# Two attention layers on one core: all softmax divisions on ScalarE, and the sums of the output weights spread out

## The chip, the cores and the metric

The kernel runs on one core of a Trainium2 chip. A core has TensorE (PE, matrix products), VectorE (DVE), ScalarE (ACT), GpSimd (POOL) and SyncE (SP, which here only issues transfers), and 16 DMA engines that they share. The time is the device time of one execution in microseconds (us); lower is better. The engines run on their own and wait for one another through semaphores.

## The reference

Four images of 32 x 32 positions and 768 channels go through two layers. Each layer normalizes its input in 32 groups of channels and adds the result of an attention over all 1024 positions with 12 heads of 64 channels and decomposed relative positions:

```python
qkv = x @ Wqkv                       # layer 1: + qkv_b
rel_h = einsum('bhwc,hkc->bhwk', r_q, Rh)
rel_w = einsum('bhwc,wkc->bhwk', r_q, Rw)
scores = scale * einsum('bqc,bkc->bqk', q, k) + rel_h[..., :, None] + rel_w[..., None, :]
attn = softmax(scores)
out = einsum('bqk,bkc->bqc', attn, v)
x = x + (out @ Wproj + bproj)        # x was normalized by _gn before the attention
```

## The kernel before

**Images, pairs, units.** The code counts eight images: 0 to 3 are the four inputs in layer 0, 4 to 7 the same four in layer 1 (`LAST` = 7). An image has six pairs of heads (`pair` 0 to 5; `g` counts pairs through all images), and a pair has eight units (g, n) of 128 query positions, n = 0 to 7. The main loop runs over these 384 units (`at` is the running number) and issues the work of all engines in one order written out by hand; nothing is reordered afterwards, so each engine goes through its instructions in the order of the program, and so do the DMA queues that SyncE and ScalarE issue to.

**A unit.** `biases` makes the sum of the two relative positions for both heads on POOL (L533, into `sc`, six buffers, two units ahead of use). `scores` multiplies k by q on TensorE (L547). `exponentials` subtracts them on VectorE with the row minimum (L559, `sm`) and takes the exponential and its row sum on ScalarE (L563). `divide` makes the reciprocal of the row sum on VectorE (L571) and multiplies `sc` by it, one instruction per head: on ScalarE (L577), or, for the first head of n = 2 and n = 4, on POOL (L575), except in the very last pair. `turn` transposes blocks on VectorE (L583) and writes the result to DRAM (`td`, L585). `read_back` fetches it again with keys on the partitions (`pt`, L594), two or three iterations later. `weigh` multiplies `pt` by v on TensorE (L612, `av`): for units 0 to 3 of a pair at n = 6, for units 4 to 7 at n = 2 of the next pair. An iteration issues the scores and the division of the next unit, the biases of the unit after that and the transpose of its own.

**Between them.** The pieces of the products for q, k, v and the output (`products`, `values`, `out_product`, L354, L382, L438, L701) are put into the units by `plans`. They are seven-product forms of 2 x 2 block products, so sums of weights and of inputs are needed: `combine` and `combine_values` (L135, L146), `sums` for the next image (L323, in pair 4 from n = 4 and in pair 5) and `out_sums` (L691), all on POOL. `complete` loads the residual, adds it on POOL (L758) and stores the result one iteration later from SyncE (L762). Relative positions go through DRAM (`tdr`) and come back as `rel` (L518).

**The sums of the output weights.** For each layer l and each of three column blocks o, `combined` loads the four blocks of the output weight from DRAM (L635), makes four differences on POOL (L640) and stores them in DRAM tables (L649), from where `fetch_out` reads them for every image (L675). With b11, b12, b21, b22 for the four blocks, table 1 is b12 - b11, table 2 is b22 - (table 1), table 3 is b22 - b12 and table 4 is b21 - (table 2). `combining` says at which unit each stage is issued: loads (stage 0) and stores (stage 3) at the top of the iteration, ahead of that iteration's read-backs and `td`; the subtractions (stages 1 and 2) near its end:

```python
    for k in range(LAYERS * NB):
        for stage in range(4):
            combining.setdefault(NT + 4 * k + stage + (stage > 0), []).append((k // NB, k % NB, stage))
```

With NT = 8 and NB = 3 these are six blocks, four units apart: block k has its loads at unit 8 + 4k, its subtractions two and three units later and its stores four units later, where the loads of block k + 1 come too. The first tables are needed in pair 4 of image 0, those of layer 1 in pair 4 of image 4. Loaded weights lie in `unit` buffers, of which there are 35, used also by inputs, attention outputs and residuals.

Of the kernel before, what the change touches and what calls it, by code (L numbers as in the profile page):

```python
# [31 lines left out]
FP = mybir.dt.float32  # L32
AF = mybir.ActivationFunctionType
ALU = mybir.AluOpType
ENGINES = {getattr(mybir.EngineType, e) for e in ("PE", "DVE", "Activation", "Pool", "SP")}

P = 128
# [4 lines left out]
NT = S // P  # L42
# [4 lines left out]
LAYERS = 2  # L47
NP = NH // 2
FULL = 2 * HW - 1
BIG = 3.0e38  # L50
NB = NC // 2
# [6 lines left out]
def attention_blocks(ctx: ExitStack, tc: tile.TileContext, a: dict, out: bass.AP):  # L58
    nc = tc.nc
# [15 lines left out]
    dram = ctx.enter_context(tc.tile_pool(name="scratch", bufs=1, space=bass.MemoryType.DRAM))  # L75
# [11 lines left out]
    NPAIR = NI * NP  # L87

    def unit(name):

        return upool.tile([P, HALF], FP, tag="u", name=name)
# [69 lines left out]
    for sign, base in ((1, 0), (-1, GS // NC - 1)):  # L161
        nc.gpsimd.affine_select(
            out=same_group, in_=same_group, pattern=[[-sign * (GS // NC), NG], [0, GS // NC]],
# [4 lines left out]
    for l in range(LAYERS):  # L168
        tab = const.tile([P, 2, 2 * HW], FP, tag=f"tab{l}", name=f"tab{l}")
        nc.gpsimd.memset(tab, 0.0)  # L170
        for i, ax in enumerate("hw"):
            src = a[f"rel{ax}{l}"]
            n = src.shape[1]
# [21 lines left out]
    for l in range(LAYERS):  # L195
        t = const.tile([P, NC], FP, tag=f"bo{l}", name=f"bo{l}")
# [370 lines left out]

    def divide(g, n):
        st = st_of[g, n]
        last = g + 1 == NPAIR  # L570
        nc.vector.reciprocal(st[:, 2, :], st[:, 1, :])  # L571
        for h in range(2):
            sc = sc_of[g, n, h].rearrange("p k j -> p (k j)")
            if h == 0 and n in (2, 4) and not last:
                nc.gpsimd.tensor_scalar(sc, sc, st[:, 2, h : h + 1], 1.0, ALU.mult, ALU.mult)  # L575
            else:
                nc.scalar.mul(sc, sc, st[:, 2, h : h + 1])  # L577

    def turn(g, n):

# [46 lines left out]
    tables = {}  # L627

    def combined(l, o, stage, held={}):

        if stage == 0:
            tables[l, o] = dram.tile([4, P, NB * P], FP, tag=f"tw{l}_{o}", name=f"tw_{l}_{o}")
            held[l, o] = [unit(f"t{k}_{l}_{o}")[:, : NB * P] for k in range(4)]
            for k, t in enumerate(held[l, o]):
                nc.sync.dma_start(  # L635
                    out=t, in_=a[f"wo{l}"][o + k % 2 * NB][:, k // 2 * NB * P : (k // 2 + 1) * NB * P]
                )
            return
        b11, b12, b21, b22 = held[l, o]
        sub = lambda to, x, y: nc.gpsimd.tensor_tensor(to, x, y, ALU.subtract)  # L640
        if stage == 1:
            sub(b11, b12, b11)
            sub(b12, b22, b12)
        elif stage == 2:
            sub(b22, b22, b11)
            sub(b21, b21, b22)
        else:
            for k, t in enumerate((b11, b22, b12, b21)):
                nc.sync.dma_start(out=tables[l, o][k], in_=t)  # L649

    order = [
        (im, kind, o) for im in range(LAST)
# [6 lines left out]
    def fetch_out(at):  # L659

        if at >= len(order):
            if at < len(order) + 2:
                fetch(3 + 4 * (at - len(order)))
            return
        im, kind, o = order[at]
        l = images[im][0]
        raw = lambda k: a[f"wo{l}"][o + k % 2 * NB][:, k // 2 * NB * P : (k // 2 + 1) * NB * P]
        made = lambda k: tables[l, o][k - 1]
        out_weights[im, kind, o] = []
        for k, src in enumerate({  # L670
            "a": lambda: (raw(0), made(3)), "b": lambda: (raw(2), made(2)),
            "c": lambda: (made(1), made(4)), "d": lambda: (raw(3),),
        }[kind]()):
            w = wopool.tile([P, NB, P], FP, tag="wo", name=f"wo_{im}_{kind}{o}_{k}")
            nc.sync.dma_start(out=w, in_=src.rearrange("p (c o) -> p c o", o=P))  # L675
            out_weights[im, kind, o].append(w)
# [91 lines left out]
    at_start, at_sums, at_stats, here = {}, {}, {}, [0]  # L768
# [136 lines left out]
        (0, 3): (1, 1, 2), (0, 1): (1, 2, 0), (0, 2): (1, 2, 1), (0, 4): (1, 2, 2),  # L905
    }
    combining = {}
    for k in range(LAYERS * NB):
        for stage in range(4):
            combining.setdefault(NT + 4 * k + stage + (stage > 0), []).append((k // NB, k % NB, stage))  # L910
    applies = {
        1: ((0, 0), (0, 3)), 2: ((0, 1), (0, 4)), 3: ((1, 0), (1, 1), (0, 2)),
        4: ((1, 3), (1, 4), (0, 5)), 5: ((1, 2), (1, 5)),
# [10 lines left out]
    with tc.manual_schedule(engines=ENGINES):  # L924
# [40 lines left out]
        ahead["G0"].part()  # L965
        ahead["G0"].between()
        divide(0, 0)
        biases(0, 1)
        held = []
# [11 lines left out]
        for at, (g, n) in enumerate(units):  # L981
# [22 lines left out]
            if (pair, n) in streams and im + 1 < B:  # L1004
                c, i = streams[pair, n]
                x = unit(f"stream_{im + 1}_{c}_{i}")
# [4 lines left out]
            for part in combining.get(at, []):  # L1011
                if part[2] % 3 == 0:
                    combined(*part)
            if (pair, n) == (4, 0) and im == 0:
                fetch_out(0)
                fetch_out(1)
# [50 lines left out]
            if at + 1 < len(units):  # L1067
                divide(*units[at + 1])
# [10 lines left out]
            if (pair, n) in out_sum_steps:  # L1079
                back, which, c = out_sum_steps[pair, n]  # L1080
                if 0 <= im - back < LAST:
                    out_sums(im - back, which, c)
            for part in combining.get(at, []):
                if part[2] % 3:
                    combined(*part)
# [79 lines left out]
```

## Time and profile before

| | |
|---|---|
| median of 3 runs | 3297.41 us (3296.28 to 3298.17) |
| profiled execution, its own time | 3294.32 us |
| span from first to last instruction | 3292.2 us, granted clock 0.998 |
| busy: PE, DVE, ACT, POOL | 3236.3, 2581.8, 2004.3, 2668.7 us |
| data moved | 1029.63 MB, mean 313 GB/s |
| L575 (divisions on POOL) | 94, 105.3 us busy |
| L640 (differences of output weights) | 24, 24.1 us busy |
| L635 and L649 (their loads and stores) | 24 and 24, 192 KB each |

A line of a group in the page reads: line of the code, engine, operation, written tile <- read tiles, shapes, count, then busy time in us and mean time of one in ns, then the time that the engine stood idle just before these instructions and what ended most of it. A line of the waits reads: who waited <- what it waited for: us in total, times, longest. A row of windows gives, for a stretch of time, the busy time of each engine with its number of instructions, the granted clock of TensorE, the busy share of the DMA engines and their rate. In the timeline a row is start, length, engine and instruction, and in brackets the idle time before it with its releaser. Busy time of TensorE is modelled from matmuls that overlap, so a stretch that is fully busy there need not run at full pace.

### The profile page before, as it was taken

To read this page: it belongs to the slowest core of one execution; us is meant where nothing else is said; L and a number is where in the kernel's file an instruction comes from. 1 tells how busy PE (TensorE), PEld (TensorE's weight loads), DVE (VectorE), ACT (ScalarE), POOL (GpSimd) and SP (SyncE) were. 2 spreads that over 40 slices of the span, in tenths; PEclk is the share of its full clock that TensorE was granted. 3 is DMA by queue.
4 is the path that set the end of the run, shared out by engine and by line. 5 is a ranking of instruction groups with operands and counts; after the bars stand their busy time and mean duration, and the time that the engine had idled before them with its cause. 6 is when DMAs were issued, how large, how long until landed. Compare 5 with 4: busy or idle time off the path is not lost.

```text
span 3292.2 us, 63898 instructions
## 1 busy us (share of the span) xinstructions
PE 3236.3 (98%) x24800; PEld 1864.7 (57%) x24800; DVE 2581.8 (78%) x4085; ACT 2004.3 (61%) x3004; POOL 2668.7 (81%) x1458
## 2 busy tenths in 40 slices
PE   8999999999999999999999999999999999999999
PEld 5555555655555555655555555655555555555554
DVE  7877777887778877878777887778877788777785
ACT  4666655566656665566656566555766567565662
POOL 6888987789877897778977889688897888878772
PEclk9999999999999999999999999999999999999999
DMA  4999988899888998889888898879898898888997
GB/s 157 344 348 349 332 304 309 322 332 323 320 310 307 345 318 302 300 308 339 316 310 289 321 341 313 298 286 340 320 333 287 291 342 313 326 286 307 334 334 256
DMA packets 386847, 1029.63 MB, mean 313 GB/s; under 512 B 31344, under 2 KB 71664, under 8 KB 337392
## 3 DMA queue, kind: packets, MB, share of 16 engines
q1 hardware_dynamic: 370992, 998.11, 84.9%
q10 hardware_dynamic: 15552, 27.43, 2.2%
q8 instruction: 196, 3.21, 0.4%
q14 instruction: 107, 0.88, 0.1%
HBM read 567.71 MB, written 457.70 MB: 311 GB/s over the span
## 4 chain that ended last, share of the span: by engine, by line
PE 77%; POOL 8%; DMA 7%; DVE 5%; issue 3%; SPq 1%; ACT 1%; POOLq 0%; DVEq 0%; ACTq 0%
PE pj L354 19%; PE s L547 16%; PE av L612 15%; PE pv L354 9%; POOL sc L533 5%; PE ob L354 3%; PE pj L382 3%; PE oa L354 3%; DMA td<-tb 3%; PE oc L354 3%; DVE tb L583 2%; PE tp L485 2%; DMA rel<-tdr 2%; PE o L815 1%; PE od L701 1%
## 5 line engine op out<-in xcount | busy, mean ns | idle before, releaser
L533 POOL TENSOR_TENSOR sc<-rel 128x1024 f32<-128x1024 f32 x768 | 1940.6, 2553 | 278.2 <-DVE tb L583 251.7
L559 DVE CUSTOM_DVE_ANT_0 sc<-s,sc 128x1024 f32<-128x1024 f32 x768 | 913.1, 1222 | 362.9 <-PE s L547 263.8
L577 ACT ACTIVATE sc<-sc,sm 128x1024 f32<-128x1024 f32 x674 | 743.4, 1143 | 635.6 <-DVE sm L571 523.8
L563 ACT ACTIVATE sc<-sc,sm 128x1024 f32<-128x1024 f32 x768 | 878.8, 1146 | 347.5 <-DVE sm L559 345.8
L583 DVE STREAM_TRANSPOSE tb<-sc 128x1024 f32<-128x1024 f32 x768 | 909.1, 1224 | 44.9 <-DMA td<-tb 43.7
L547 PE MATMUL s<-k,q 64*128 64x512 f32 x3072 | 741.9, 596 | 1.5 <-DVE sm L559 0.8
L612 PE MATMUL av<-pt,v 128*64 128x256 f32 x6144 | 691.7, 383 | 19.1 <-DMA pt<-td 18.0
L612 PEld LDWEIGHTS av<-pt,v 128*64 128x64 f32 x6144 | 437.8, 138 | 302.4 <-issue 56.7
L547 PEld LDWEIGHTS s<-k,q 64*128 64x128 f32 x3072 | 288.4, 187 | 299.1 <-issue 263.7
L575 POOL TENSOR_SCALAR sc<-sc,sm 128x1024 f32<-128x1024 f32 x94 | 105.3, 1120 | 242.9 <-DVE sm L571 242.3
L354 PEld LDWEIGHTS pv<-wv,xn 64*128 64x128 f32 x4608 | 270.7, 188 | 40.4 <-issue 25.3
L354 PE MATMUL pv<-wv,xn 64*128 64x128 f32 x4608 | 274.5, 272 | 3.3 <-DVE wv L343 3.2
L354 PE MATMUL pj<-xn,wa 64*128 64x512 f32 x1152 | 265.4, 593 | 7.8 <-DVE oy L718 5.2
L354 PE MATMUL pj<-s,wc 64*128 64x512 f32 x576 | 264.2, 592 | 2.3 <-DVE wc L343 2.3
L354 PE MATMUL pj<-xn,w 64*128 64x512 f32 x1152 | 264.5, 591 | 0.8 <-DVE k L398 0.7
L354 PE MATMUL pj<-s,w 64*128 64x512 f32 x576 | 264.2, 592 | 0.0
L354 PEld LDWEIGHTS pj<-xn,wa 64*128 64x128 f32 x1152 | 110.8, 187 | 145.1 <-issue 115.3
L354 PEld LDWEIGHTS pj<-xn,w 64*128 64x128 f32 x1152 | 114.3, 187 | 135.4 <-issue 128.6
L456 DVE TENSOR_TENSOR v<-pv,v 128x512 f32<-128x512 f32 x216 | 140.0, 685 | 56.4 <-ACT v L458 40.9
L508 ACT COPY rel<-raw 32x256 f32<-32x256 f32 x384 | 154.9, 403 | 7.9 <-DMA rel<-tdr 3.2
L490 ACT COPY t<-tp 128x512 f32<-128x512 f32 x96 | 56.1, 585 | 156.5 <-PE tp L485 156.5
L354 PEld LDWEIGHTS pv<-wv,s 64*128 64x128 f32 x2304 | 137.1, 188 | 24.2 <-issue 16.9
(134 smaller groups left out, 3497.1 us busy)
## 6 DMA issues: line engine op xcount, KB each, us to landing
td<-tb SPq DMA_DIRECT2D x384, 1024.0 KB, 5.6
pt<-td SPq DMA_DIRECT2D x382, 1024.0 KB, 8.3
tdr<-t ACTq DMA_DIRECT2D x96, 256.0 KB, 4.8
wa<-in_wqk SPq DMA_DIRECT2D x48, 384.0 KB, 4.4
wc<-in_wqk SPq DMA_DIRECT2D x48, 384.0 KB, 6.2
wv<-in_wv SPq DMA_DIRECT2D x24, 768.0 KB, 11.7
xn<-in_x SPq DMA_DIRECT2D x48, 256.0 KB, 6.1
res<-in_x SPq DMA_DIRECT2D x48, 256.0 KB, 5.6
```

Of the source, the lines that this page charges most:

```text
L354: nc.tensor.matmul(to, lhsT=w, rhs=x, start=at == half == 0, stop=at == 0 and half == 1)
L382: nc.tensor.matmul(t[:, h, :], lhsT=w[rows, c, :], rhs=x[c][rows, :], start=(c == 0), stop=(c == NB - 1),)
L456: add = lambda to, x, y: nc.vector.tensor_tensor(to, x, y, ALU.add)
L508: nc.scalar.copy(rel[rows], raw[rows, :, :, WIDE - 1 - HW - y : WIDE - 1 - y])
L533: nc.gpsimd.tensor_tensor(sc.rearrange("p (a k) (u l) -> p a (k u) l", a=4, l=8), rel[:, h, m, :].unsqueeze(1).unsqueeze(3).to_broadcast(s ...
L547: nc.tensor.matmul(ps[h][:, cols], lhsT=q[rows, n * P : (n + 1) * P], rhs=k[rows, cols], start=True, stop=True,)
L559: nc.vector.tensor_tensor_reduce(out=sc, in0=ps[h], in1=sc, scale=-scale, scalar=BIG, op0=ALU.add, op1=ALU.min, accum_out=st[:, 0, h : h + 1],
L563: nc.scalar.activation(sc, sc, AF.Exp, bias=st[:, 0, h : h + 1], scale=-1.0, accum_out=st[:, 1, h : h + 1],)
L575: nc.gpsimd.tensor_scalar(sc, sc, st[:, 2, h : h + 1], 1.0, ALU.mult, ALU.mult)
L577: nc.scalar.mul(sc, sc, st[:, 2, h : h + 1])
L583: nc.vector.transpose(tb[:, :, h, :], sc_of[g, n, h])
L612: nc.tensor.matmul(av[rows, at * 2 * P : (at + 1) * 2 * P], lhsT=v_of[g][:, k, rows], rhs=pt_of[g, quarter].rearrange("p n r k h i -> p (n ...
```

## The change

All divisions are issued on ScalarE, the second head's after the first's. Layer 0's three blocks of weight sums are issued ten units apart, beginning two units later: loads at units 10, 20 and 30, subtractions two and three units later, stores four units later. Layer 1's twelve sums are made one by one in images 3 and 4, at n = 1 and 4 of pair 0, n = 2 of pair 1, n = 4 of pair 2, n = 2 of pair 3 and n = 0 of pair 4. The new function `single` loads the two operands of one sum (an earlier sum from its table, where it is one), subtracts two iterations later on POOL and stores the result at the start of the iteration after that.

```diff
     def divide(g, n):
         st = st_of[g, n]
-        last = g + 1 == NPAIR
         nc.vector.reciprocal(st[:, 2, :], st[:, 1, :])
         for h in range(2):
             sc = sc_of[g, n, h].rearrange("p k j -> p (k j)")
-            if h == 0 and n in (2, 4) and not last:
-                nc.gpsimd.tensor_scalar(sc, sc, st[:, 2, h : h + 1], 1.0, ALU.mult, ALU.mult)
-            else:
-                nc.scalar.mul(sc, sc, st[:, 2, h : h + 1])
+            nc.scalar.mul(sc, sc, st[:, 2, h : h + 1])
...
+    def single(l, o, which):
+        if (l, o) not in tables:
+            tables[l, o] = dram.tile([4, P, NB * P], FP, tag=f"tw{l}_{o}", name=f"tw_{l}_{o}")
+        raw = lambda k: a[f"wo{l}"][o + k % 2 * NB][:, k // 2 * NB * P : (k // 2 + 1) * NB * P]
+        made = lambda k: tables[l, o][k - 1]
+        x, y = (unit(f"t{k}_{l}_{o}_{which}")[:, : NB * P] for k in range(2))
+        for to, at in zip((x, y), {
+            1: lambda: (raw(1), raw(0)), 2: lambda: (raw(3), made(1)),
+            4: lambda: (raw(2), made(2)), 3: lambda: (raw(3), raw(1)),
+        }[which]()):
+            nc.sync.dma_start(out=to, in_=at)
+        at_sums.setdefault(here[0] + 2, []).append(
+            lambda: nc.gpsimd.tensor_tensor(x, x, y, ALU.subtract)
+        )
+        at_start.setdefault(here[0] + 3, []).append(
+            lambda: nc.sync.dma_start(out=made(which), in_=x)
+        )
...
-    for k in range(LAYERS * NB):
-        for stage in range(4):
-            combining.setdefault(NT + 4 * k + stage + (stage > 0), []).append((k // NB, k % NB, stage))
+    for k in range(NB):
+        for stage, after in enumerate((0, 2, 3, 4)):
+            combining.setdefault(NT + 2 + 10 * k + after, []).append((0, k, stage))
+    singles = [(0, 3), (1, 3), (2, 3), (0, 1), (0, 2), (0, 4), (1, 1), (1, 2), (2, 1), (2, 2), (1, 4), (2, 4)]
+    singles = {
+        ((3 + k // 6) * NP + p) * NT + n: made
+        for k, (made, (p, n)) in enumerate(zip(singles, 2 * [(0, 1), (0, 4), (1, 2), (2, 4), (3, 2), (4, 0)]))
+    }
...
+            if at in singles:
+                made = singles[at]
+                at_start.setdefault(at, []).append(lambda made=made: single(LAYERS - 1, *made))
```

## The prediction

> **What bounds the kernel now.** The page comes first: TensorE is busy for 98% of the span, and of the three engines beside it GpSimd (POOL) is the fullest.
>
> ```profile
> PE 3236.3 (98%) x24800; PEld 1864.7 (57%) x24800; DVE 2581.8 (78%) x4085; ACT 2004.3 (61%) x3004; POOL 2668.7 (81%) x1458
> ...
> L533 POOL TENSOR_TENSOR sc<-rel 128x1024 f32<-128x1024 f32 x768 | 1940.6, 2553 | 278.2 <-DVE tb L583 251.7
> ...
> L577 ACT ACTIVATE sc<-sc,sm 128x1024 f32<-128x1024 f32 x674 | 743.4, 1143 | 635.6 <-DVE sm L571 523.8
> ...
> L575 POOL TENSOR_SCALAR sc<-sc,sm 128x1024 f32<-128x1024 f32 x94 | 105.3, 1120 | 242.9 <-DVE sm L571 242.3
> ```
>
> The last line holds one half of the change: 94 divisions of 1.12 us on POOL, before which POOL stood idle for 242.3 us until VectorE's reciprocal was there.
>
> So what can be won is only where TensorE doesn't run at its own pace. I measured that by steps: from the timeline I took the start of each unit's score matmuls (L547). TensorE's order is fixed, so the same mixture of matmuls returns in every image, and the shortest time of a step elsewhere is its floor. Step 7 of a pair (scores, then 64 `av` matmuls) takes 8.87 us almost everywhere; in pairs 1, 2 and 3 of image 0 it takes 15.26, 15.12 and 12.97. Summed over their eight steps, the floors of pairs 1 to 5 of image 0 are 56.1, 58.8, 56.1, 61.4 and 61.3 us. The windows, cut at the starts of pairs (us, then busy time of PE, PEld, DVE, ACT, POOL, clock, DMA share, GB/s), give what they took:
>
> ```profile
> 101.28:166.82 65.54, 59.85 (x454) 34.59 (x452) 49.99 (x79) 40.36 (x63) 56.81 (x33) 0.97 0.93 332
> 166.82:232.57 65.75, 61.50 (x502) 37.81 (x500) 49.41 (x78) 39.61 (x61) 55.01 (x31) 0.97 0.97 344
> 232.57:297.68 65.11, 59.36 (x454) 34.42 (x453) 48.37 (x77) 39.85 (x60) 55.72 (x34) 0.97 0.95 335
> 297.68:362.82 65.14, 62.18 (x514) 37.38 (x512) 51.44 (x90) 50.67 (x76) 57.19 (x35) 1.00 1.02 382
> ...
> 766.79:830.29 63.50, 62.14 (x478) 36.14 (x476) 49.18 (x77) 41.43 (x62) 62.95 (x37) 1.00 0.87 310
> ```
>
> Excess over the floors: 9.5, 7.0, 9.0 and 3.8 us in pairs 1 to 4 of image 0, together **29.3 us**. The last row is pair 5 of image 1: 2.2 us over its floor, and POOL busy for 62.95 of 63.50 us. That pair takes 63.5 us in each of images 1 to 6 (64.1 in image 0), whichever step the delay falls in: there **POOL is the bound**, by 2.2 us, six times 2.2 and once 2.8, **16 us**. The rest of images 1 to 7 lies within about 2 us per image of its floor.
>
> What happens in image 0 is seen in the waits of 101 to 298 us (all engines, then SyncE's queue) and in the timeline of POOL, SyncE and TensorE:
>
> ```profile
> PE av L612 <- DMA pt<-td: 13.7, 5, 4.1
> POOL sc L533 <- DMA rel<-tdr: 11.8, 3, 4.5
> POOL sc L575 <- DVE sm L571: 11.4, 3, 4.4
> ...
> SPq L649 <- POOL t L640: 14.9, 5, 6.7
> ```
>
> ```profile
> 123.53 1.12 POOL L575 TENSOR_SCALAR sc<-sc,sm 128x1024 f32<-128x1024 f32 x1 [4.29 <-DVE sm L571]
> ...
> 129.78 5.05 POOL L533 TENSOR_TENSOR sc<-rel 128x1024 f32<-128x1024 f32 x2 [3.09 <-DMA rel<-tdr]
> ...
> 139.28 8.13 SPq L649 DMA_DIRECT2D tw<-t  x4
> ...
> 161.53 5.36 PE L612 MATMUL av<-pt,v 128*64 128x256 f32 x32 [2.58 <-DMA pt<-td]
> ```
>
> Read downwards: POOL waits 4.3 us for a reciprocal, then 3.1 for a small transfer, and from there runs without a gap; SyncE stands 8.1 us over four stores of weight sums, because POOL hasn't made them; the read-back of `pt` queued behind them comes late, and TensorE waits.
>
> [...]
>
> **The change, part by part.** The orders of TensorE and VectorE stay as they are.
>
> *Divisions.* POOL loses 94 x 1.12 = 105 us and 242 us of waiting in line; ScalarE gains 94 x 1.143 = 107 us, going from 61% to 64%. In pair 5 two divisions (2.2 us) lie in POOL's gapless stretch, and one (1.1 us, with 1.25 us of waiting) at its beginning in pair 4: 3.4 to 4.6 us freed against an excess of 2.2. All of it should go; next late would be VectorE's small reductions ahead of `wa` and `wc`. I take 2.0 of each: **-14 us** over seven images (bounds -7 and -16). VectorE also waits 97.7 us in 93 places for L533, 82 us of it in the steps 4, after the division of n = 2; TensorE feels this as 0.6 us in step 4 of pair 2 and 0.23 in step 5 of pairs 1 and 3 of some images, 6 us in all: **-3 us** (0 to -6). On ScalarE the first half's division now comes before the second's, so `exp` of the next unit starts up to 1.15 us later; VectorE has 2 score passes (2.4 us) between reciprocal and transpose, which covers it, and all other steps already have both divisions there. If the cover fails at a few places: **+1 us** (0 to +6).
>
> *Weight sums in image 0.* Before, six blocks of 4 loads, 4 subtractions (1.00 us each) and 4 stores, 192 KB each, went through units 8 to 32; stores of one block and loads of the next met at units 12, 20 and 28, straight ahead of the read-backs that steps 15, 23 and 31 need. Now three blocks lie at 10, 20 and 30. Between units 8 and 34, 24 of 48 transfers (4.7 MB[...]) and 12 of 24 subtractions (12 us of POOL) leave, and with the divisions of these pairs (8 x 1.12) POOL gets 21 us, beside the 11.4 of waiting. A store now meets a read-back only at unit 24, four loads only at 20. Pairs 1 to 3 moved 66.2 MB; without 4.7 MB that is 61.5[...]. [...] Pair 4 (24.9 MB, the new image's `xn`) stays at its DMA rate, hardly better. Of the 29.3 us I leave 1.5, 1.5 and 2.5 in pairs 1 to 3[...], and 5 in pair 4 (no better than now, with a little carried over): 10.5 stay, 18.8 go, **-18 us** rounded against me (bounds -7 and -29).
>
> *Weight sums of layer 1.* Twelve singles in images 3 and 4: 24 loads, 12 subtractions, 12 stores; 12 loads and 2.4 MB more than before, as b22 and earlier sums are fetched again. POOL's 12 us there lie in steps where it has gaps (6.1 us in step 3 of pair 4). On SyncE's queue 36 issues of 0.45 us are spread over 800 us. Each store waits for POOL one step after the subtraction, as `complete`'s store at L762 does: those waited 58 times, 3.4 us on average, 7.5 at most. Behind them stand `td`, `pt` and `rel`. In images 3 and 4 the read-backs land 2.9 to 20 us before their first matmul, but for one per image (last of pair 4, 0.0 to 0.1 us), which no store of a single precedes directly. **+2 us** (0 to +10).
>
> Sum: -14 - 3 + 1 - 18 + 2 = **-32 us**. The profiled execution took 3294.32 us (span 3292.2 and 2.1 around it), so 3262.3; the median shown lies 3.1 us above that execution: **3265 us**.
>
> **Rivals.** (1) *DMA keeps image 0.* If pairs 1 to 4 merely shrink with their bytes at the old average of 340 GB/s and new waits on `pt` eat half, 7 us come there: -14 - 3 + 3 - 7 = -21, 3276 us. For it: shares of 0.93 to 0.97. Against: in windows of 10 us the rate falls to 256 GB/s at 130 to 140 us, where SyncE's queue stood behind VectorE and POOL: the engines weren't full just ahead of the longest delay. (2) *POOL's wait only changes its name.* The next L533 waits for VectorE's transpose (251.7 us already); if that comes no earlier, pair 5 keeps its length: -18 + 3 = -15, 3282 us. Against: 62.95 of 63.50 us busy leave no wait to rename. (3) *Slower: singles block SyncE.* If each store stands 7.5 us where the read-back behind has 3 of slack, 12 x 4.5 = 54 us stand in the place of the 2 above: -34 + 54 = +20, 3317 us. It decides from 34 / 12 = 2.8 us per single. Against: only stores at steps 3, 4 and 7 stand right ahead of a read-back, and POOL is earlier than before. That the change doesn't do what it says is excluded by the order of instructions: 94 divisions are on ScalarE.
>
> **Chances.** Forecast 0.70, rival 1 0.15, rival 2 0.10, rival 3 0.03, other 0.02. The range reaches from all excess of pair 5 and image 0 gone (-16 - 3 - 29 = -48) to just past rival 2: 3249 to 3284 us. A measurement can tell 0.2% (6.6 us) from no change: faster 0.93, same 0.04, slower 0.03.
>
> **What would show it.** Right: no L575 on POOL; steps 7 of pairs 1 to 3 of image 0 near 9 to 11 us; pair 5 near 61.5 us with gaps on POOL; VectorE's wait for L533 far below 97 us; images 3 and 4 no longer than 5 and 6. Wrong: pair 5 still at 63.5, image 0's pairs still near 65, or `av` waiting for `pt` in images 3 and 4.

## The result, and the profile after

The kernel after takes **3247.64 us** in the median (3246.09 to 3248.93), beside 3297.79 us for the kernel before on the same chip (3296.28 to 3300.32): a ratio of 0.9847, 95% interval 0.9834 to 0.986. It is 50 us faster; forecast were 32, and the result lies just below the lower end of the range.

The page of the kernel after (busy time and share; the chain that ended last; two groups):

```profile
PE 3217.2 (99%) x24800; PEld 1855.8 (57%) x24800; DVE 2577.8 (79%) x4085; ACT 2093.8 (64%) x3098; POOL 2571.7 (79%) x1364
...
PE 93%; DMA 3%; DVE 2%; issue 1%; SPq 0%; ACT 0%; POOL 0%; DVEq 0%; POOLq 0%
...
L533 POOL TENSOR_TENSOR sc<-rel 128x1024 f32<-128x1024 f32 x768 | 1944.4, 2559 | 535.7 <-DVE tb L579 420.5
L573 ACT ACTIVATE sc<-sc,sm 128x1024 f32<-128x1024 f32 x768 | 841.0, 1143 | 588.0 <-DVE sm L570 472.9
```

No division is left on POOL, and ScalarE's group of divisions has grown from 743.4 to 841.0 us, at an unchanged 1.143 us each (two that follow each other overlap a little: at 155.82 us two take 2.19 us together). The chain is the quickest reading: TensorE now makes up 93% of it, where it was 77% before, and POOL has fallen from 8% to nothing. POOL itself is not idle for less time than before. Its wait for VectorE's transpose ahead of L533 grew from 251.7 to 420.5 us, while the 242.3 us of waiting for the reciprocal are gone. So the waiting did change its name, as the second rival said, but it no longer costs TensorE anything, and that is what the time goes by.

The windows of the kernel after, cut at its own starts of pairs (us, then busy time of PE, PEld, DVE, ACT, POOL, clock, DMA share, GB/s); pairs 1 to 4 of image 0 and pair 5 of image 1, as before:

```profile
102.36:160.12 57.76, 56.85 (x455) 33.38 (x453) 48.59 (x77) 41.93 (x64) 49.23 (x27) 1.00 0.98 349
160.12:219.20 59.08, 59.08 (x503) 36.14 (x501) 48.86 (x77) 41.27 (x63) 47.24 (x23) 1.00 0.97 339
219.20:279.31 60.11, 57.07 (x454) 33.90 (x452) 49.61 (x79) 41.78 (x63) 51.90 (x28) 1.00 0.96 349
279.31:345.34 66.03, 62.30 (x514) 36.68 (x513) 51.72 (x90) 52.41 (x79) 58.19 (x34) 1.00 1.00 373
745.18:806.92 61.74, 61.52 (x478) 35.21 (x476) 49.17 (x77) 43.44 (x64) 59.47 (x34) 1.00 0.89 320
```

Against the floors (56.1, 58.8, 56.1, 61.4) the four pairs of image 0 are over by 1.7, 0.3, 4.0 and 4.6 us, 10.6 in all; 10.5 were left there by the forecast. (The 56.1 us of pairs 1 and 3 come out only with step 1 at 6.97 us; in all profiles of this document it takes at least 7.60 there, and step 7 at least 9.13, so 0.9 us in each of the two was, as far as these profiles show, never to be had.) The clock is 1.00 where it was 0.97. That is a part of the gain: in before, the 32 `av` matmuls behind three of TensorE's five waits for `pt` (2.58, 4.08 and 2.63 us) took 5.36, 5.36 and 5.10 us at a granted clock of 0.68, 0.68 and 0.71, and behind the other two (1.71 and 2.68 us) 3.67 us at 1.00. Two of the five:

```profile
126.65 3.67 PE L612 MATMUL av<-pt,v 128*64 128x256 f32 x32 [1.71 <-DMA pt<-td]
...
227.28 5.36 PE L612 MATMUL av<-pt,v 128*64 128x256 f32 x32 [4.08 <-DMA pt<-td]
```

Together this is 4.8 us (an estimate, from the differences to 3.67) that these waits cost beyond their own length.

Pair 5 of image 1 went from 63.50 to 61.74 us (floor 61.3), with 2.3 us of gaps on POOL. In image 0 the waits of 101 to 298 us that had 13.7, 11.8 and 11.4 us now read:

```profile
POOL sc L533 <- DMA rel<-tdr: 19.8, 3, 7.2
...
POOL sc L533 <- DVE tb L579: 7.3, 4, 5.3
...
PE av L608 <- DMA pt<-td: 2.9, 2, 2.4
```

TensorE's wait for `pt` is down by 10.8 us; POOL's wait for `rel` has grown by 8, without TensorE waiting longer. In the timeline a store of weight sums that took SyncE 8.13 us is now

```profile
129.57 10.08 POOL L533 TENSOR_TENSOR sc<-rel 128x1024 f32<-128x1024 f32 x4 [7.22 <-DMA rel<-tdr]
...
156.19 3.56 SPq L645 DMA_DIRECT2D tw<-t  x4
```

without a stop for POOL. All three steps 7 of pairs 1 to 3 take 9.13 us (15.26, 15.12, 12.97 before).

The steps from score start to score start, summed by place and set beside the forecast (profiled execution after, less before):

| place | forecast | measured |
|---|---|---|
| pair 5 of images 0 to 6 | -14 | -14.3 |
| VectorE's waits for L533: pairs 1 to 3 of images 1 to 7 | -3 | -8.4 |
| image 0, pairs 1 to 4 | -18 | -18.6 |
| step 0 of pair 4, images 1 to 6 | 0 | -5.4 |
| cover on ScalarE and the singles | +3 | 0 |
| start of the program (+1.1) and the rest | 0 | +1.3 |
| profiled execution | -32 | -45.4 |
| from there to the median | +3.1 | -1.3 |

The last row needs a word. The one profiled execution of before (3294.32 us) lies 3.5 us below the median that was measured beside the kernel after, and that of after (3248.93) 1.3 above its own. Differences between profiles below therefore understate a gain over the kernel before by some 3.5 us, and by what the other profile lies above its own median. From image 1 on, profiles of kernels that are the same there mostly agree to 0.2 us per pair (0.7 at most). Image 0 varies more: in two kernels below that are the same as before up to step 7 of its pair 3, single steps ahead of that took up to 1.8 us more or less than in before, and in two others that are the same as each other there, one step took 15.74 and 11.10 us.

### The profile page after: what moved, and what is told of

Read it like the earlier page. It is cut to its first block, busy times and chain, and to the rows that moved or that the text cites. A ratio compares the mean times of both kernels' runs of the same rounds, so it can differ in the third digit from the quotient of the medians.

```text
span 3246.9 us, 64020 instructions
## 1 busy us (share of the span) xinstructions
PE 3217.2 (99%) x24800; PEld 1855.8 (57%) x24800; DVE 2577.8 (79%) x4085; ACT 2093.8 (64%) x3098; POOL 2571.7 (79%) x1364
## 4 chain that ended last, share of the span: by engine, by line
PE 93%; DMA 3%; DVE 2%; issue 1%; SPq 0%; ACT 0%; POOL 0%; DVEq 0%; POOLq 0%
PE pj L354 22%; PE s L547 20%; PE av L608 20%; PE pv L354 11%; PE pj L382 4%; PE oa L354 3%; PE ob L354 3%; PE oc L354 3%; PE tp L485 2%; PE pv L438 2%; PE od L716 2%; PE o L830 1%; DMA td<-tb 1%; DMA xn<-in_x 1%; DVE tb L579 1%
## 5 line engine op out<-in xcount | busy, mean ns | idle before, releaser
L533 POOL TENSOR_TENSOR sc<-rel 128x1024 f32<-128x1024 f32 x768 | 1944.4, 2559 | 535.7 <-DVE tb L579 420.5
L573 ACT ACTIVATE sc<-sc,sm 128x1024 f32<-128x1024 f32 x768 | 841.0, 1143 | 588.0 <-DVE sm L570 472.9
L563 ACT ACTIVATE sc<-sc,sm 128x1024 f32<-128x1024 f32 x768 | 877.3, 1144 | 257.2 <-DVE sm L559 251.5
L579 DVE STREAM_TRANSPOSE tb<-sc 128x1024 f32<-128x1024 f32 x768 | 911.3, 1230 | 18.6 <-DMA td<-tb 17.5
L608 PE MATMUL av<-pt,v 128*64 128x256 f32 x6144 | 684.7, 381 | 2.9 <-DMA pt<-td 2.9
L354 PEld LDWEIGHTS pj<-s,wc 64*128 64x128 f32 x576 | 105.7, 187 | 69.4 <-issue 64.2
```

Of the source, the lines that this page charges most:

```text
L354: nc.tensor.matmul(to, lhsT=w, rhs=x, start=at == half == 0, stop=at == 0 and half == 1)
L533: nc.gpsimd.tensor_tensor(sc.rearrange("p (a k) (u l) -> p a (k u) l", a=4, l=8), rel[:, h, m, :].unsqueeze(1).unsqueeze(3).to_broadcast(s ...
L563: nc.scalar.activation(sc, sc, AF.Exp, bias=st[:, 0, h : h + 1], scale=-1.0, accum_out=st[:, 1, h : h + 1],)
L579: nc.vector.transpose(tb[:, :, h, :], sc_of[g, n, h])
L608: nc.tensor.matmul(av[rows, at * 2 * P : (at + 1) * 2 * P], lhsT=v_of[g][:, k, rows], rhs=pt_of[g, quarter].rearrange("p n r k h i -> p (n ...
```

## Experiments: which half does what

**The divisions alone.** The kernel before with the new `divide`, and its six blocks as they were:

```diff
-            if h == 0 and n in (2, 4) and not last:
-                nc.gpsimd.tensor_scalar(sc, sc, st[:, 2, h : h + 1], 1.0, ALU.mult, ALU.mult)
-            else:
-                nc.scalar.mul(sc, sc, st[:, 2, h : h + 1])
+            nc.scalar.mul(sc, sc, st[:, 2, h : h + 1])
```

> The kernel before with all divisions on ScalarE and the weight sums left as they were. My theory (two separate gains): pair 5 of images 0 to 6 loses its 2 us each (14 us), the small steps and step 0 of pair 4 lose 8 and 5 us, since they hang on when POOL works; image 0's pairs 1 to 4 gain only what POOL's freedom gives, about 6 us, since 48 transfers stay. Together some 33 us, near 3265 us. Rival (POOL's wait for the reciprocal alone made SyncE and the read-backs late): image 0 gains nearly all of its 18.6 us here, near 3252 us.

Measured: 3269.02 us, ratio 0.9913 (0.9899 to 0.9928).

**The sums alone.** The kernel after with the old `divide`.

> The changed kernel with the divisions of n = 2 and 4 back on POOL. My theory: pair 5 stays at 63.5 us and the small steps stay long; image 0's pairs 1 to 3 gain 12 to 15 us by 24 fewer transfers and 12 fewer subtractions; near 3284 us. Rival (the sums moved little, the divisions did it): less than 6 us gained, 3292 us or more.

Measured: 3281.29 us, ratio 0.9952 (0.9937 to 0.9967).

By place, against the profile of before: with the divisions alone pair 5 gains 13.8 us, VectorE's places 8.4 and step 0 of pair 4 5.5, all that the kernel after has there; image 0, where some 6 us were expected, gains nothing (+4.5 in pairs 1 to 4, most of it in two steps of pair 3, where single executions differ). With the sums alone image 0 gains 18.9 us, also the whole amount (12 to 15 were expected in pairs 1 to 3). So the two halves split by place. The windows of both, pairs 1 to 3 of image 0, first the divisions alone:

```profile
100.62:166.55 65.93, 59.57 (x455) 34.62 (x453) 49.94 (x79) 42.47 (x65) 55.30 (x31) 0.97 0.93 330
166.55:231.49 64.94, 61.31 (x502) 37.80 (x501) 49.48 (x78) 41.55 (x63) 52.19 (x29) 0.97 0.98 348
231.49:300.36 68.87, 61.46 (x455) 36.43 (x453) 49.86 (x81) 42.02 (x63) 54.40 (x32) 0.93 0.94 332
```

and the sums alone (the same three, and pair 5 of image 1):

```profile
100.56:157.56 57.00, 56.64 (x455) 33.48 (x453) 48.81 (x77) 39.87 (x61) 50.89 (x29) 1.00 0.96 353
157.56:217.58 60.02, 59.67 (x502) 36.39 (x501) 48.22 (x77) 39.51 (x62) 50.41 (x25) 1.00 0.95 330
217.58:278.09 60.51, 57.12 (x454) 33.92 (x453) 50.05 (x79) 39.64 (x59) 53.60 (x30) 1.00 0.96 350
...
746.79:810.33 63.54, 62.18 (x479) 36.25 (x477) 49.12 (x77) 41.49 (x62) 62.99 (x37) 1.00 0.86 311
```

In the last row POOL is as full as it was before (62.99 of 63.54 us). SyncE's waits tell what image 0 hangs on. Between 101 and 298 us it stood 14.9 us before, 6.7 at most, over stores of weight sums that POOL hadn't made; with the divisions alone it still does:

```profile
SPq L646 <- POOL t L637: 10.5, 5, 4.8
```

With the sums alone no such wait in image 0 is longer than 0.7 us. So the link that the forecast read from the timeline, stores ahead of the read-back of `pt`, is the right one; what makes POOL late with the sums is not its wait for reciprocals.

What the sums alone also show is a price that the kernel after doesn't pay: pair 1 of image 3 and pair 3 of images 3 and 4 are longer than before by 2.15, 3.71 and 3.74 us, **9.6 us**, the slow rival's mechanism on a small scale. SyncE's waits there, and below them those of the kernel after:

```profile
SPq L781 <- POOL res L777: 184.5, 57, 7.5
SPq L667 <- POOL t L664: 14.6, 5, 4.1
```

```profile
SPq L777 <- POOL res L773: 47.3, 28, 4.2
...
SPq L663 <- POOL t L660: 3.3, 2, 1.8
```

With the divisions on POOL, five stores of singles hold SyncE's queue for 14.6 us, 4.1 at most; without them two, for 3.3 us. The divisions' move pays for the singles.

## Experiments: the waiting or the work

POOL lost two things with the divisions, 105 us of work and 242 us of waiting in line. Each was put back by itself.

**The wait kept.** The kernel after, with one POOL operation on a single column where each division was, which waits for the reciprocal as it did:

```diff
         for h in range(2):
             sc = sc_of[g, n, h].rearrange("p k j -> p (k j)")
+            if h == 0 and n in (2, 4) and g + 1 < NPAIR:
+                nc.gpsimd.tensor_scalar(st[:, 0, h : h + 1], st[:, 2, h : h + 1], 1.0, 1.0, ALU.mult, ALU.mult)
             nc.scalar.mul(sc, sc, st[:, 2, h : h + 1])
```

> The changed kernel, with a one-column multiplication of the reciprocal on POOL at the place of each of the 94 divisions: POOL waits in line as before, but has next to nothing to do. If the waiting cost what the steps 4 and 5 and step 0 of pair 4 gained, 10 to 14 us come back (3258 to 3262 us), with pair 5 at 61.3 to 61.7 us still, since POOL had no wait there. Rival (the work counted, not the wait): within 3 us of the changed kernel, 3251 us at most.

Measured: 3258.39 us, ratio 0.9879 (0.9865 to 0.9894).

**The work kept.** The kernel after, with two POOL products of a 128 x 192 scratch tile in the same place, which wait for nothing:

```diff
+                for _ in range(2):
+                    nc.gpsimd.tensor_tensor(idle, idle, idle, ALU.mult)
```

> The changed kernel, with two POOL multiplications of 128x192 (an estimated 0.54 us each, from the lengths of 384 and 512 columns) on a tile of their own at the place of each division: POOL has the work, but doesn't wait for the reciprocal. If pair 5 was bound by POOL's work, it comes back to about 63 us in images 0 to 6 (9 to 13 us, 3257 to 3261 us), with step 4 of pair 2 still at 7.08 us. Rival (the waits did it all): within 3 us of the changed kernel.

Measured: 3249.50 us, ratio 0.986 (0.9843 to 0.9876).

Put back alone, the wait costs 11 us and the work 2, and the 2 are within the noise. The 11 us of the wait lie within the expected 10 to 14, but hardly where they were expected: step 0 of pair 4 gives back 0.7 us, step 4 of pair 2 nothing, and pair 5, which was to stay within 61.7 us, takes up to 62.9. Of the work, 9 to 13 us were expected by the first theory, and it failed. Neither gives back what the divisions on POOL cost, 34 us between the sums alone (3281.29) and the kernel after: some 20 of them appear only when wait and work come together. The page of the kernel with the work kept, and the waits of the one with the wait kept:

```profile
PE 3215.9 (99%) x24800; PEld 1853.3 (57%) x24800; DVE 2578.6 (79%) x4085; ACT 2093.9 (64%) x3098; POOL 2662.6 (82%) x1553
```

```profile
POOL sc L533 <- DVE tb L581: 259.7, 93, 6.5
POOL sm L574 <- DVE sm L570: 251.5, 64, 6.2
```

POOL is busy for 2662.6 us in the first, nearly as long as before the change (2668.7; the products put back took 96.4 us, the divisions 105.3), and yet pair 5 stays at its floor but for 1.6 us in image 0. The second is POOL's old pattern of waits (252 for the transpose, 242 for the reciprocal) with little of the work. It costs 2.7 us in pair 5, 1.9 in image 0 and 4.7 in pair 3 of images 3 and 4, where stores of singles wait for POOL again. So the words "POOL is the bound" in pair 5 were too coarse. Before, wait and work together put it 2.2 us over; taking away either brings the pair to its floor or within 1.6 us of it. Of the two alone the waiting does more harm, about half of it through the stores of singles.

## Experiments: the weight sums

**No singles.** The kernel after, with layer 1 reading layer 0's tables: its 24 loads, 12 subtractions and 12 stores are left out, and its output weights are layer 0's sums.

```diff
-            if at in singles:
+            if at in singles and at % NT == 1 and at // NT % NP == 0:
+                for k in range(NB):
+                    tables[1, k] = tables[0, k]
+            if False:
```

> The changed kernel without the twelve single sums: layer 1 takes layer 0's tables, so its output weights are wrong, and 24 loads, 12 subtractions and 12 stores are left out. If they lie wholly beside other work, as images 3 and 4 suggest, it is within 1.5 us of the changed kernel. If they cost what the prediction charged (2 us) or more, images 3 and 4 get shorter by that.

Measured: 3249.56 us, ratio 0.9852 (0.9835 to 0.9868). Images 3 and 4 are within 0.2 us per pair of the kernel after. The singles cost nothing there.

**Three blocks, close together.** The kernel after with layer 0's blocks four units apart, at 8, 12 and 16:

```diff
-            combining.setdefault(NT + 2 + 10 * k + after, []).append((0, k, stage))
+            combining.setdefault(NT + 4 * k + after, []).append((0, k, stage))
```

> The changed kernel with layer 0's three blocks four units apart again, from unit 8 on (loads at 8, 12 and 16, stores at 12, 16 and 20). If the amount of transfers and subtractions per pair sets image 0, pairs 1 and 2 get longer by 3 to 8 us together, pair 3 shorter by 2 to 4: 0 to 5 us slower than the changed kernel. Rival (only the sum over the image counts, the places don't): within 1.5 us, with pairs 1 to 3 as long as before within 1 us each.

Measured: 3256.64 us, ratio 0.9872 (0.9858 to 0.9887). Pairs 1 and 2 of image 0, then 3 and 4:

```profile
101.08:167.76 66.68, 59.55 (x455) 34.62 (x453) 49.86 (x79) 42.50 (x65) 55.28 (x31) 0.97 0.92 326
167.76:229.46 61.70, 59.55 (x503) 36.79 (x501) 46.96 (x75) 40.90 (x62) 48.76 (x26) 1.00 0.94 333
229.46:287.74 58.28, 57.12 (x454) 33.91 (x452) 50.08 (x79) 41.75 (x63) 48.28 (x24) 1.00 0.96 350
287.74:352.33 64.59, 62.02 (x514) 36.76 (x513) 52.04 (x90) 53.14 (x80) 54.31 (x30) 1.00 1.00 368
```

This is 9 us slower than the kernel after, where 0 to 5 were expected. Pair 1, with two blocks in it, is back at 66.7 us, with step 7 at 15.8, and pair 2 is 2.6 us longer; pairs 3 and 4, now free of blocks, are 1.8 and 1.4 us shorter than in the kernel after. By places, of the 18.6 us gained in image 0, 10.3 come with half of the blocks gone to layer 1, at the old distance, and 8.3 with the distance. In pair 1 SyncE stands again over stores for which POOL isn't ready (101 to 298 us):

```profile
SPq L645 <- POOL t L636: 5.4, 3, 5.0
```

In the fourteen profiles step 7 of pair 1 takes 14.97 to 16.10 us where a store of weight sums waits 4.8 us or more for `t` in image 0, and 9.13 to 10.46 where none waits longer than 0.8. The DMA share of the bad pair is the lowest of the four (0.92), so it isn't late because the DMA engines were full throughout. Which part of a block makes POOL late, its loads or its subtractions, was not tried.

**The blocks earlier.** The kernel after with the blocks at units 2, 12 and 22:

```diff
-            combining.setdefault(NT + 2 + 10 * k + after, []).append((0, k, stage))
+            combining.setdefault(2 + 10 * k + after, []).append((0, k, stage))
```

> The kernel after with the three blocks of weight sums of the first layer's output eight units earlier: they begin at units 2, 12 and 22 of image 0, not at 10, 20 and 30; all else as after. If what is left over in image 0 (4 us in pair 3, 4.7 in pair 4) comes from the last block's loads and stores at units 30 to 34, pair 3 loses 2 to 4 us and pair 4 1 to 3, and pair 0, where GpSimd and the DMA engines have room, gains none: -4 us, 3244. Rival: pair 4 is late from the new image's xn alone, and what pair 3 loses comes back in pairs 1 and 2, which get a second block: 0 to +4 us, 3248 to 3252.

Measured: 3251.81 us, ratio 0.9861 (0.9848 to 0.9875). Pair 3 gains 2.2 us and pair 4 1.4, as the first theory had it, but pair 1 loses 6.1 (step 3 at 15.74 us) and pair 2 1.2. The rival was right that what pair 3 loses comes back earlier. In pair 1 it comes by another way, with a single block: no store waits longer than 1.0 us for POOL, and step 3 is late, not step 7. So it isn't only the number of blocks in a pair that counts, but where each one lies, and what sets the best place was not worked out further.

## Experiments: step 0 of pair 4

Nothing in the forecast covered the 5.4 us at this step. In the trace of before, small operations of the group norm on VectorE stand out there, by shape:

```profile
L277 DVE TENSOR_SCALAR turned<-nrm 128x32 f32<-128x32 f32 x14 | 10.3, 733 | 0.5
L282 DVE COPY turned<-means 128x2 f32<-128x2 f32 x7 | 7.1, 1019 | 0.0
```

A copy of two columns has a mean of 1.02 us. The timeline of before at this step in image 5, VectorE's three rows and POOL's:

```profile
2306.25 5.07 POOL L533 TENSOR_TENSOR sc<-rel 128x1024 f32<-128x1024 f32 x2
2309.28 2.07 DVE L282 COPY turned<-means 128x2 f32<-128x2 f32 x1
...
2311.85 0.18 DVE L277 TENSOR_SCALAR turned<-nrm 128x32 f32<-128x32 f32 x1
...
2312.64 5.04 POOL L533 TENSOR_TENSOR sc<-rel 128x1024 f32<-128x1024 f32 x2
2315.84 1.87 DVE L277 TENSOR_SCALAR turned<-nrm 128x32 f32<-128x32 f32 x1
```

TensorE pays for this later in the step, where it waits for VectorE's `oy` (L718), which stands behind these operations in VectorE's order:

```profile
2320.43 2.85 PE L354 MATMUL pj<-xn,wa 64*128 64x512 f32 x12 [1.19 <-DVE oy L718]
```

The copy ends at 2311.35, 0.03 us after POOL's pair of L533 (2311.32), and the last `tensor_scalar` at 2317.71, 0.03 after the next pair (2317.68); the one in between, while POOL is free, takes 0.18. So it goes in five of images 1 to 6. In image 2 no small operation is stretched (0.14 and 0.18 us) and the step still takes 11.46 us: there VectorE had waited 2.13 us for a store that held `tb`, and TensorE then waits 0.8 us for the reduction of `wo_c`. So the stretched operations end with L533, and a `tensor_reduce` in the same stretch did not: the one of L276, just ahead of the last `tensor_scalar`, took 0.18 us from 2315.63 on, with L533 running. What holds the stretched ones, and whether they would pass as reductions, these times don't show. Four kernels were made to test whether L533 is what they stand for, and the first two turned out to test something else.

**On ScalarE.** The kernel before, and the kernel after, with the copy and the `tensor_scalar` moved off VectorE:

```diff
-            nc.vector.tensor_scalar(
-                by_group(to), total.unsqueeze(2).to_broadcast([P, HW // n, n]), 1.0 / n, None, ALU.mult
-            )
+            nc.scalar.mul(by_group(to), total.unsqueeze(2).to_broadcast([P, HW // n, n]), 1.0 / n)
...
-            nc.vector.tensor_copy(w0[:, :2], means[:, im, :])
+            nc.scalar.copy(w0[:, :2], means[:, im, :])
```

> The kernel before, with the small copy at L282 and the small multiplication at L277 of the next image's normalization on ScalarE instead of VectorE; nothing else changes. Theory (VectorE's small copy and multiplication stand until POOL's running instruction ends): step 0 of pair 4 comes down from 11.5 to 11.9 us to near 10.44 in images 1 to 6, 6 to 8 us in all, near 3290 us. Rival (my reading in the prediction, that VectorE simply has too much to do there): 2 of 2.5 us of work at most leave VectorE where they were long, but 0.3 us where they were short, and step 0 of pair 4 stays above 11 us; less than 2 us in all.

> The changed kernel with the same two small operations on ScalarE. Theory: images 1 and 2, where L277 still takes 1.45 us, lose 1.05 us each in step 0 of pair 4; the others stay at 10.44 us: 2 us, near 3245.5 us. Rival: no difference.

Measured: 3324.32 us, ratio 1.0077 (1.0062 to 1.0092), and 3276.45 us, 0.9935. They are 27 and 29 us slower than the kernels that they start from, and the reason lies elsewhere. In the first kernel's timeline of image 5:

```profile
2335.90 1.15 ACT L561 ACTIVATE sc<-sc,sm 128x1024 f32<-128x1024 f32 x1
...
2337.03 1.65 ACT L506 COPY rel<-raw 32x256 f32<-32x256 f32 x4
2338.70 0.23 ACT L277 ACTIVATE turned<-nrm 128x32 f32<-128x32 f32 x1
```

The operation itself takes 0.23 us, but it stands behind exponentials and copies in ScalarE's queue, and VectorE waited 3.19 us for it. Neither theory is tested by that: the edit replaced one wait with another.

**As reductions, still on VectorE.** The kernel before with the same two operations as `tensor_reduce` of the same shapes, in the same places; the factor 1/4 goes to POOL as two products of 128 x 32:

```diff
-            nc.vector.tensor_scalar(
-                by_group(to), total.unsqueeze(2).to_broadcast([P, HW // n, n]), 1.0 / n, None, ALU.mult
-            )
+            nc.vector.tensor_reduce(
+                by_group(to), total.unsqueeze(2).to_broadcast([P, HW // n, n]).unsqueeze(3), mybir.AxisListType.X, ALU.max
+            )
...
-            nc.vector.tensor_copy(w0[:, :2], means[:, im, :])
+            nc.vector.tensor_reduce(w0[:, :2], means[:, im, :].unsqueeze(2), mybir.AxisListType.X, ALU.max)
...
+            nc.gpsimd.tensor_scalar(w0, w0, 1.0 / n, 1.0, ALU.mult, ALU.mult)
             nc.gpsimd.tensor_tensor(w1, w1, w0, ALU.subtract)
             nc.gpsimd.tensor_tensor(w1, w1, w1, ALU.mult)
+            nc.gpsimd.tensor_scalar(w1, w1, 1.0 / n, 1.0, ALU.mult, ALU.mult)
```

(The text below puts POOL's two products at 128 x 128; they are 128 x 32.)

> The kernel before, with VectorE's two kinds of small operations of the group norm that had taken up to 2 us (the copy of 128x2 and the tensor_scalar of 128x32) written as tensor_reduce of the same size, still on VectorE and in the same places; the factor 1/4 moves to GpSimd, as two more small operations of 128x128 per image. Theory A (a small copy or tensor_scalar of VectorE can't end while GpSimd's L533 runs[...]): none of these operations is longer than 0.5 us, step 0 of pair 4 goes from 11.5-11.9 to 10.4-10.6 us in images 1 to 6, 7 to 8 us in all: 3290, ratio 0.9977. Rival B (what made them long was the queue and order of VectorE, or memory traffic, and any operation there ends with L533): the reductions also end with L533, up to 2 us each, and step 0 of pair 4 stays at 11.5 us: 3298, ratio 1.000.

Measured: 3291.87 us beside 3297.88, ratio 0.998 (0.9974 to 0.9987): 6 us faster. The groups by shape and the timeline at the same place of image 5:

```profile
L277 DVE TENSOR_REDUCE turned<-nrm 128x32 f32<-128x32 f32 x14 | 2.6, 186 | 0.5
...
L282 DVE TENSOR_REDUCE turned<-means 128x2 f32<-128x2 f32 x7 | 0.9, 134 | 0.0
```

```profile
2306.11 5.09 POOL L535 TENSOR_TENSOR sc<-rel 128x1024 f32<-128x1024 f32 x2
2309.17 0.14 DVE L282 TENSOR_REDUCE turned<-means 128x2 f32<-128x2 f32 x1
...
2312.30 5.05 POOL L535 TENSOR_TENSOR sc<-rel 128x1024 f32<-128x1024 f32 x2
2315.71 0.19 DVE L277 TENSOR_REDUCE turned<-nrm 128x32 f32<-128x32 f32 x1
```

POOL does the same work at nearly the same times (and two more products of 0.22 us per image), the shapes and places on VectorE are the same, and 2.07 and 1.87 us became 0.14 and 0.19. Step 0 of pair 4 falls to 10.44 us in five of images 1 to 6 (11.14 in image 2), 6.9 us in all. Theory A holds for these operations, and the time follows. Image 2, which was late for another reason, stays late, as it should. (The profiled execution itself is only 2.1 us shorter than that of before: pair 3 of image 0 took 5.1 us more in it. That isn't the edit's doing: TensorE's wait for `pt` in step 7 was 3.65 us, not 2.68, and ended at 296.56 us, the first edited instruction starts at 301.32, and the 32 matmuls behind the wait took 6.52 us, not 3.67.)

**The same on the kernel after.**

> The kernel after with the same edit of the group norm. Theory A: step 0 of pair 4 goes from 11.5 to 10.45 us in images 1 and 2, where a tensor_scalar still took 1.45 us, and stays in images 3 to 6: -2 us against the kernel after, 3246 us, ratio 0.984. Rival B: no change, 3248 us. If moving the factor to GpSimd delays L533, the steps 7 and 0 of pair 4 grow in all images, by less than 1 us each.

Measured: 3245.57 us (3243.57 to 3249.21), ratio 0.9844 (0.9831 to 0.9858). Step 0 of pair 4 takes 10.44 us in images 1 to 6, and images 1 and 2 gain 1.06 and 1.04 us, as theory A said. Against the kernel after the median is 2 us lower, but the two were timed beside before in different sets and the intervals overlap, so the gain is placed by the trace and not settled by the times. This is the best version that was run.

**Both, with the earlier blocks.**

> Both edits on the kernel after: earlier blocks of weight sums, and the group norm's small operations as reductions. If both are worth what they are alone and don't meet, their gains add: -6 us against the kernel after, 3242 us, ratio 0.983; if the earlier blocks only move the delay, 3246 to 3250.

Measured: 3247.51 us, ratio 0.9848 (0.9835 to 0.9862). The gains that were expected to add don't: the earlier blocks, which alone brought none, bring none here either, and pair 1 of image 0 pays for them again (+2.8 us, with step 3 at 11.10).

## Why the prediction was right in part, and where it failed

**The step that failed** is the price of what lies outside pair 5 and image 0. "The rest of images 1 to 7 lies within about 2 us per image of its floor", some 14 us in seven images, went into the sum with 3 us, and the lower end of the range had no more for it. The runs show 13.8 us there, 8.4 where VectorE waits for L533 and 5.4 in step 0 of pair 4, and the divisions alone bring all of it (8.4 and 5.5). Term by term:

- **Pair 5, -14 us: right in size, by two errors that cancel.** -14.3 measured, and -13.8 by the divisions alone. In images 1 to 4 step 1 takes 7.46 us in every profile, before and after, so the floor there is 61.74, not 61.3, and the whole excess was 14.4, not 16. All of it went; the 2.0 of 2.2 that the forecast took, because small reductions would be late next, came out right by chance. The bound was shared by work and waiting, too, and the forecast's price (3.4 to 4.6 us freed against 2.2) held because either would nearly have done.
- **Image 0, -18 us: right, with half of its reasons.** -18.6 measured, and 10.6 us left over where 10.5 were forecast. So close a match is in part luck: what was left over was the author's estimate, and kernels that are the same as the kernel after in nearly all of these pairs gain 17.2 (no singles) and 20.2 us (reductions). It comes from the sums alone; that POOL loses eight divisions and 11.4 us of waiting there, which the forecast counted in, brought nothing. The link by SyncE's stores was right. The first rival, DMA at its old average, had 7 us here and falls; the close blocks show that the distance between blocks counts beside their number.
- **VectorE's waits for L533, -3 us: mis-sized, -8.4 measured.** The forecast found 6 us in these places by its own steps and then took half, for no reason that the profile gave. All of it went: 4.5 us in step 4 of pair 2, 1.9 in step 5 of pairs 1 and 3, and 1.6 more in three steps of image 2, of which it isn't shown that they hang on L533. The wait on VectorE (80.8 us of it in the steps 4) fell from 97.7 us to

```profile
DVE sc L559 <- POOL sc L533: 19.1, 19, 1.7
```

- **Step 0 of pair 4, 0 us: missed.** -5.4 measured. The sum put none of the 2 us per image on this step. VectorE's small reductions, which the forecast names as late next in pair 5, are themselves short here too (0.14 us). In the kernel before, a copy and a `tensor_scalar` near them stood until POOL's L533 had ended, and with the divisions gone POOL runs through these places earlier: the copy now takes 0.13 to 0.20 us in all images; the `tensor_scalar` still took some 1.45 us in images 1 and 2, where the step stays at 11.5 us. The mean of 1.02 us for a copy of two columns stood in the profile of before. The experiment with reductions shows the cause in all images but image 2; that POOL's earlier phase is what the change brings is read from the traces and wasn't tried by itself. Put back alone, the wait returns 0.7 of these 5.4 us and the work none.
- **Costs of +3 us: not there.** The cover on ScalarE held everywhere, and the singles cost nothing once POOL doesn't wait for reciprocals. With the divisions on POOL they cost 9.6 us, so the reason given, that POOL is earlier than before, was the right one. The third rival needed 2.8 us per single; the largest wait of a store is 1.8 us.
- **From the profiled execution to the median, +3.1 us: -1.3.** A profile is one execution, and these two lay on opposite sides of their medians. With the 13.4 us by which the terms above and the start differ from their forecasts, this 4.4 makes up the distance to the forecast.

Together, the two large terms came out within 1 us, in part by luck, and those that the forecast set by discretion, half of 6 us here, nothing there and +3 for costs, were where it lost.

## What to carry to other kernels

Price a stage by its excess over the shortest time of the same step elsewhere, after making sure that the step holds the same work there, and give every excess its place in the sum: a part left out needs a row of the profile that says what will keep it. When an operation is moved off an engine, count its work and what queued behind its wait together, since most of their price here (some 20 of 34 us) came only from both, and look for what pays indirectly, such as stores on another queue. Look through the groups by shape for tiny operations with a mean far above that of others of their size: here a copy of 128x2 had 1.02 us, and as a reduction 0.13, and no list of waits showed what it stood for.

## What the runs showed of the hardware

- **Two small VectorE operations stood until a long `tensor_tensor` of GpSimd had ended, and a `tensor_reduce` of the same shape did not.** The copy of 128x2 took 0.13 to 0.20 us when free and up to 2.07 us beside L533, the `tensor_scalar` of 128x32 0.18 and up to 1.87; as reductions in the same places they took 0.13 to 0.15 and 0.19. The time is shown as busy, not as a wait: nothing in the waits points to it, only that the end falls 0.02 to 0.04 us behind GpSimd's. Not every such operation stands: in the kernel with reductions a `tensor_scalar` of 128x1 took 0.21 us with GpSimd's `tensor_tensor` running, and the copies of 128x512 that read `av` took 0.69 us beside it and without it.
- **Here a wait in line did more harm than work that waits for nothing.** With 2662.6 us busy and no wait for the reciprocal the kernel took 3249.50 us; with 2584.6 us busy and that wait, 3258.39. With both on POOL it was 3281.29, more than the two prices together.
- **Three short waits of TensorE cost more than their length.** Behind waits of 2.58, 4.08 and 2.63 us the same 32 matmuls took 5.36, 5.36 and 5.10 us in place of 3.67, at a granted clock of 0.68, 0.68 and 0.71; behind one of 2.68 us they took 3.67, at 1.00. These lengths alone don't say which wait is followed by the lower clock.
